# An adjacency-masked two-layer residual network on one core: the last group's work written out as one list of pieces

## The chip, the core and the metric

The kernel runs on one core of a Trainium2 chip. The core has five engines that work side by side, each through its own stream of instructions in order: TensorE (PE, matrix products; its weight loads are shown as PEld), VectorE (DVE), ScalarE (ACT), GpSimd (POOL) and SyncE (SP, which here issues the DMA transfers). An instruction that waits holds up everything behind it on its engine. The metric is the device time of one execution in microseconds (us); lower is better.

## What is computed

There are 128 graphs ("batches") of 128 nodes with 512 features each, and one 128x128 adjacency matrix per graph. Both layers are applied to every batch, each with a residual and a layer norm:

```python
# layer 0: 8-head attention under the adjacency mask
q, k, v = (x @ W + b for each of Wq, Wk, Wv)          # 128x512 @ 512x512
logits = einsum('bqhd,bkhd->bhqk', q, k) / sqrt(64)
attn = softmax(where(adj > 0, logits, -1e9), axis=-1)
out = einsum('bhqk,bkhd->bqhd', attn, v) @ Wo + bo
x = layernorm(x + relu(out))
# layer 1: additive graph attention, softmax over the first node index
Wh = x @ W1
e = leaky(s_i[:, :, None] + s_j[:, None, :])          # s_i, s_j = Wh @ a1, Wh @ a2
att = softmax(where(adj > 0, e, -9e15), axis=1)
x = layernorm(x + leaky(att @ Wh))
```

All of it is float32. The batches don't depend on each other; within a batch everything is one long chain.

## The kernel before

**Tiles and products.** Four batches form a group. The Q, K and V products of a group (`products`, L371) and the two 512x512 products of a pair of batches (`pair_product`, L420, for the output projection with `wo` and for `W1`) are done by one level of Strassen's scheme: seven products of half size, p1, p5, p6, p2, p7, p4, p3 (`strassen`, L283). Three of them (p1, p6, p7) are copied out of the accumulator banks by ScalarE into the tiles `t0`, `t2`, `t3` (`st_t` for a group, `pr_t` for a pair, L443), since the bank is then written again by the next product; VectorE adds these to the banks to form the blocks of the result. The block sums of the left operand are made on GpSimd (`left_blocks`, L269, four operations, L276 to L279).

**A batch's way.** Layer 0: scores (L476, banks `lg`), mask added and maximum taken on VectorE (L485, L491), eight exponentials and eight divisions on ScalarE (`exp` L497, `divide` L511, tile `pa`), the result stored to DRAM (L518) and fetched back in another order by four transfers (L522, tile `paz`), turned on VectorE (L526, `paT`), the product with V (`attend`, L539), copied to `oT` on ScalarE (L552), the projection with `wo` for the pair, the residual (L586) and the norm. The norm is `norm_stats` (L565: statistics on VectorE, L567 and L569, then the inverse root on GpSimd, L572 and L574) and `normalize` (L577: one VectorE operation, L578). The normalized tile `x1` is stored (L594), fetched back by four transfers (L240), turned on VectorE (L245, `x1T`). Layer 1: the product with `W1` for the pair, the edge softmax (`EdgeSoftmax`, L645: two turns on TensorE, L652 and L653, then L655 to L672 on ScalarE and VectorE), the product with the attention (L681), a copy to `z` on ScalarE (L685), leaky and residual on VectorE (L689, L690), a norm of the same kind (L578) and the store of the output (L697).

**Order.** All engines run in the order in which the program is written (`manual_schedule`, L710). A software pipeline sets it: step `t` of the loop at L782 does the first softmax of batch `t`, the attention product of batch `t-1`, the output projection of the pair that begins at `t-3` (odd `t`) or the `W1` product of the pair at `t-6` (even `t`), the edge softmax of batch `t-7`, the end of batch `t-8`, and a few pieces of the Q, K, V products of a later group (`group_steps`), which are all done by the end of step 124. The loop runs to `t = 136`, 128 batches and 9 steps more; in the last steps whatever has no batch left is skipped, and the rest keeps its order and place in the step.

**Buffers.** Tiles come from pools with a few buffers per name. In the stretch of interest: one buffer each for `pa`, `paz`, `paT`, `oT`, `x1T`, `z`, `y` and for each of the three copies `pr_t`; one for `e`, two for `att`, three for the small statistics; five accumulator banks for `lg`, `p_oT`, `p_e`, `p_h` and the pair products, three more for the group products.

Of the kernel before, what the change touches and what calls it, by code (L numbers as in the profile page):

```python
# [8 lines left out]
F32 = mybir.dt.float32  # L9
# [15 lines left out]
def kernel(  # L25
# [206 lines left out]
    X, XT, XS, Q, K, V, MF, PA, OT, X1T, X1, WH, ATT = ({} for _ in range(13))  # L232
# [31 lines left out]
    def sum_x(g):  # L264
        sums = big.tile([P, 3, 2, 2 * P], F32, name="xS")
        XS[g], add = left_blocks(XT[g], sums)
        return add

    def left_blocks(xT, sums):  # L269


        xt = xT.rearrange("p (i c) (h t) -> p i h c t", i=2, h=2)
        a11, a12, a21, a22 = (xt[:, i, h] for h in range(2) for i in range(2))

        def add():
            nc.gpsimd.tensor_add(sums[:, 0], a21, a22)  # L276
            nc.gpsimd.tensor_sub(sums[:, 1], sums[:, 0], a11)
            nc.gpsimd.tensor_sub(sums[:, 2], a11, a21)
            nc.gpsimd.tensor_sub(a21, a12, sums[:, 1])  # L279

        return (a11, a12, a21, a22, sums[:, 0], sums[:, 1], sums[:, 2]), add

    def strassen(bank, multiply, read, add):  # L283

        p, t = {}, {}

        def p1():  # L290
            p["y"] = bank("y")
            multiply(p["y"], 0, True)
            t[0] = read("t0", p["y"], 0)

        def p5():
            p["w"] = bank("w")
            multiply(p["w"], 4, True)

        def p6():
            multiply(p["y"], 5, False)  # L300
            t[2] = read("t2", p["y"], 1)

        def p2():
            p["x"] = bank("x")
            multiply(p["x"], 1, True)
            add(0, 0, p["x"], t[0])

        def p7():
            multiply(p["y"], 6, False)
            t[3] = read("t3", p["y"], 1)  # L310
            add(1, 1, p["w"], t[3])

        def p4():
            multiply(p["y"], 3, False)
            add(1, 0, p["y"], None)

        def p3():
            multiply(p["w"], 2, False)
            add(0, 1, p["w"], t[2])

        return [p1, p5, p6, p2, p7, p4, p3]
# [49 lines left out]
    def products(g):  # L371
# [20 lines left out]
        chains = [  # L392
# [3 lines left out]
        ]  # L396

# [20 lines left out]
        return order + chains[2][5:]  # L418

    def pair_product(xs, w, add, bias=None):  # L420
# [3 lines left out]
        def multiply(p, n, start):  # L424
# [6 lines left out]
            for kc in range(2):  # L431
                nc.tensor.matmul(  # L432
                    p[:, :width],
                    xs[n][:, kc, :],
                    w[:, PLACE[n], kc, :],
                    start=start and kc == 0,
                    stop=True,
                    skip_group_check=True,
                )

        def read_out(name, p, o):
            t = work.tile([P, HALF + 1], F32, name=f"pr_{name}")
            nc.scalar.copy(t[:, :width], p[:, :width])  # L443
            return t[:, :width]

        return strassen(
            lambda role: psum(f"p_{role}"),
# [17 lines left out]
    class Softmax:  # L465


        def __init__(self, b):
            self.b = b
            q, k = (a[b // GROUP, b % GROUP // 2] for a in (Q, K))  # L470
# [9 lines left out]
        def maxima(self):  # L480
            self.pa = work.tile([P, 4, H, 32], F32, name="pa")
            by_head = self.pa.rearrange("p b h k -> p h b k")
            mf = MF[self.b].rearrange("p (b k) -> p b k", b=4)
            for r in range(2):
                nc.vector.tensor_add(  # L485
                    by_head[:, r * NC : (r + 1) * NC],
                    self.lg[r].rearrange("p c (b k) -> p c b k", b=4),
                    mf.unsqueeze(1).to_broadcast([P, NC, 4, 32]),
                )
            self.nmax = small.tile([P, H], F32, name="nmax")  # L490
            nc.vector.tensor_reduce(self.nmax, by_head, AX.XY, ALU.max, negate=True)  # L491
            self.sums = small.tile([P, H], F32, name="sums")
            self.rs = small.tile([P, H], F32, name="rs")
# [21 lines left out]
        def spread(self):  # L515

            d = dram.tile([P, 4, H * 32], F32, name="pa_dram")
            nc.sync.dma_start(d, self.pa.rearrange("p b h k -> p b (h k)"))  # L518
            self.paz = work.tile([P, 4, H * 32], F32, name="paz")
            block = d.rearrange("(a i) b e -> b i a e", i=32)  # L520
            for k in range(4):
                nc.sync.dma_start(self.paz[32 * k : 32 * k + 32], block[k])  # L522

        def transpose(self):
            self.paT = work.tile([P, H, P], F32, name="paT")
# [5 lines left out]
    def attend(sm):  # L531

        b = sm.b
        v = V[b // GROUP, b % GROUP // 2][:, b % 2, :]
        p = psum("p_oT").rearrange("p (c q) -> p c q", c=NC)
        for c in range(NC):
            for r in range(2):
                h = 2 * c + r
                nc.tensor.matmul(  # L539
                    p[r * HD : (r + 1) * HD, c, :],  # L540
                    v[:, h * HD : (h + 1) * HD],
                    sm.paT[:, r * NC + c, :],
                    start=True,
                    stop=True,
                )
        pair, h = divmod(b, 2)

        def copy():
            if h == 0:
                OT[pair] = work.tile([P, NC, 2 * P], F32, name="oT")  # L550
            for c in range(NC):
                nc.scalar.activation(  # L552
                    OT[pair][:, c, h * P : (h + 1) * P],
                    p[:, c, :],
# [3 lines left out]
            if h == 1:  # L558
                sums = work.tile([P, 3, 2, P], F32, name="oS")
                OT[pair], add = left_blocks(OT[pair], sums)  # L560
                add()

        return copy

    def norm_stats(src):  # L565
        st = small.tile([P, 6], F32, name="st")
        nc.vector.bn_stats(st, src)  # L567
        mv = small.tile([P, 2], F32, name="mv")
        nc.vector.bn_aggr(mv, st)  # L569
        with tc.high_priority(offset=400):  # L570
            ve = small.tile([P, 1], F32, name="ve")
            nc.gpsimd.tensor_scalar_add(ve, mv[:, 1:2], EPS)  # L572
            rstd = small.tile([P, 1], F32, name="rstd")
            nc.gpsimd.tensor_tensor(rstd, ve, mhalf, ALU.pow)  # L574
        return mv[:, 0:1], rstd

    def normalize(dst, stats):  # L577
        nc.vector.tensor_scalar(dst, dst, stats[0], stats[1], ALU.subtract, ALU.mult)  # L578

    def project_o(pair):  # L580

        y = {}

        def residual(b, o, src):
            dst = X1[b][:, o * HALF : (o + 1) * HALF] if o is not None else X1[b]
            nc.vector.scalar_tensor_tensor(dst, src, 0.0, dst, op0=ALU.max, op1=ALU.add)  # L586

        stats, d = {}, {}

        def store(h):  # L590
            b = 2 * pair + h
            normalize(X1[b], stats[h])
            d[h] = dram.tile([P, D], F32, name="x1_dram")
            nc.sync.dma_start(d[h], X1[b])  # L594

        def spread_both():
            store(0)
            for h in (1, 0):
                X[2 * pair + h, 1] = spread(d[h])

        def add(h, o, p, t):
            b = 2 * pair + h
            if h == 0:
                if o == 0:
                    y[0] = work.tile([P, D], F32, name="y")
                nc.vector.tensor_add(y[0][:, o * HALF : (o + 1) * HALF], p, t)
                if o == 1:
                    residual(b, None, y[0])
                    stats[0] = norm_stats(X1[b])
                    store(1)  # L610
                    later.append(spread_both)
            elif o == 1:
                nc.vector.tensor_add(t, p, t)
                residual(b, 1, t)
            else:
                residual(b, 0, p)
                stats[1] = norm_stats(X1[b])

        return pair_product(OT.pop(pair), wo, add, bias_rows)

    def transpose_x1(b):
        pair, h = divmod(b, 2)
        if h == 0:
            X1T[pair] = work.tile([P, NC, 2 * P], F32, name="x1T")
        transpose_blocks(X1T[pair][:, :, h * P : (h + 1) * P], X.pop((b, 1)))
        if h == 1:
            sums = work.tile([P, 3, 2, P], F32, name="x1S")
            X1T[pair], add = left_blocks(X1T[pair], sums)
            add()

    def project_w(pair):

        for h in range(2):
            WH[2 * pair + h] = work.tile([P, 2, HALF + 1], F32, name="wh", bufs=4)

        def add(h, o, p, t):
            dst = WH[2 * pair + h][:, o, :]
            if t is None:
                nc.scalar.copy(dst, p)
            else:  # L640
                nc.vector.tensor_add(dst, p, t)  # L641

        return pair_product(X1T.pop(pair), w1, add)

    class EdgeSoftmax:  # L645


        def __init__(self, b):
            self.b = b
            s = WH[b][:, :, HALF : HALF + 1]  # L650
            self.p = psum("p_e").rearrange("p (c k) -> p c k", c=NC)
            nc.tensor.transpose(self.p[:, 0, :], s[:, 0, :].to_broadcast([P, P]), ident)  # L652
            nc.tensor.transpose(self.p[:, 1, :], MF.pop(b), ident)  # L653
            self.e = small.tile([P, P], F32, name="e", bufs=1)
# [273 lines left out]
```

## Time and profile before

| | us |
|---|---|
| median of 3 runs | 2503.51 (2501.39 to 2504.53) |
| the profiled execution | 2503.92 |
| its span, first to last instruction | 2502.1 |
| first scores of batch 124 on TensorE (L476) start at | 2359.49 |
| scores of batches 125, 126, 127 start at | 2379.53, 2393.67, 2410.37 |
| last product (L681) starts at | 2492.49 |

The span counts from the first instruction to the last; the device time lies 1.8 us around it. From 2359.5 us on, the last group's first scores, there are 142.6 us left. Busy time in that stretch: PE 99.03, DVE 92.88, ACT 55.11, POOL 39.23 us. A record of "x8" on TensorE is eight passes; a float32 product is shown as two passes, so "x4" of L432 is one of the seven products of a pair.

### The profile page before, as it was taken

Reading aid. Unit: us, or ns where it says so; the run is one execution under the profiler, and the core shown is the slowest. Engines: PE = TensorE matmul, PEld = TensorE weight load, DVE = VectorE, ACT = ScalarE, POOL = GpSimd, SP = SyncE. Lnnn points to the kernel's source line nnn. Section 1 sums busy time; section 2 is a strip of 40 time slices with the busy share of each in tenths; the row PEclk is TensorE's granted clock in tenths of the full one; section 3 lists DMA queues with packets and bytes.
Section 4 is the critical chain, followed back from the end, with each engine's and each line's share of the span. In section 5 each row is a group of like instructions: output and inputs, shape, how many; then the busy total and the mean of one; then the engine's idle time right before and its main releaser. Section 6 shows DMA issues by size and latency. Waiting matters only on the chain.

```text
span 2502.1 us, 43770 instructions
## 1 busy us (share of the span) xinstructions
PE 2438.1 (97%) x13713; PEld 2006.4 (80%) x13713; DVE 1815.5 (73%) x3757; ACT 1429.1 (57%) x5188; POOL 779.0 (31%) x1161
## 2 busy tenths in 40 slices
PE   8899999999999999999999999999999999999975
PEld 6688888888888888888888888888888888888853
DVE  6667776777776777776777777777777777777675
ACT  2565565565565565556566556556556556556551
POOL 2222323322323323323323323323333323333232
PEclk9999999999999999999999999999999999999987
DMA  6544544544544544544544544544544444544441
GB/s 191 179 140 143 164 154 144 170 151 144 162 146 156 168 149 146 165 146 151 169 145 152 164 144 152 168 145 150 166 149 152 163 144 152 164 150 147 151 133 47
DMA packets 351112, 379.92 MB, mean 152 GB/s; under 512 B 38936, under 2 KB 255008, under 8 KB 350880
## 3 DMA queue, kind: packets, MB, share of 16 engines
q1 hardware_dynamic: 350016, 376.07, 46.9%
q8 instruction: 110, 1.80, 0.3%
q10 hardware_dynamic: 864, 1.05, 0.1%
q14 instruction: 122, 1.00, 0.1%
HBM read 240.91 MB, written 136.05 MB: 151 GB/s over the span
## 4 chain that ended last, share of the span: by engine, by line
PE 93%; DVE 2%; issue 1%; ACT 1%; DMA 1%; POOL 1%; SPq 0%; POOLq 0%; DVEq 0%; ACTq 0%
PE st_y L349 26%; PE p_y L432 17%; PE st_w L349 13%; PE p_w L432 9%; PE st_x L349 7%; PE lg L476 5%; PE p_oT L539 5%; PE p_h L681 4%; PE p_x L432 4%; PE p_e L653 1%; PE p_e L652 1%; DMA wv_n<-wv 1%; ACT pa L497 0%; DVE st L567 0%; ACT pa L511 0%
## 5 line engine op out<-in xcount | busy, mean ns | idle before, releaser
L572 POOL TENSOR_SCALAR ve<-mv 128x1 f32<-128x1 f32 x256 | 68.5, 267 | 1376.1 <-DVE mv L569 1376.1
L497 ACT ACTIVATE pa<-pa,nmax 128x128 f32<-128x128 f32 x1024 | 398.9, 392 | 47.6 <-DVE nmax L491 36.4
L511 ACT ACTIVATE pa<-pa,rs 128x128 f32<-128x128 f32 x1024 | 336.5, 395 | 30.0 <-DVE rs L507 30.0
L552 ACT ACTIVATE oT<-p_oT,b_cols 128x128 f32<-128x128 f32 x512 | 145.3, 366 | 201.5 <-PE p_w L432 199.4
L485 DVE TENSOR_TENSOR pa<-lg,mf 128x512 f32<-128x512 f32 x256 | 164.4, 684 | 99.4 <-PE lg L476 96.9
L326 ACT COPY st_t<-st_y 128x512 f32<-128x512 f32 x192 | 110.6, 576 | 157.4 <-PE st_y L349 157.4
L476 PEld LDWEIGHTS lg<-kT,qT 64*128 64x128 f32 x2048 | 124.3, 188 | 93.6 <-issue 93.6
L497 ACT ACTIVATION_READ_ACCUMULATOR pa<-pa,nmax 128x1 f32 x1024 | 194.1, 190 | 0.0
L574 POOL TENSOR_TENSOR rstd<-ve,mhalf 128x1 f32<-128x1 f32 x256 | 176.5, 690 | 21.3
L443 ACT COPY pr_t<-p_y 128x256 f32<-128x256 f32 (+1 forms) x384 | 140.3, 365 | 71.0 <-PE p_y L432 67.6
L526 DVE STREAM_TRANSPOSE paT<-paz 128x1024 f32<-128x1024 f32 x128 | 159.3, 1245 | 1.0 <-issue 0.3
L491 DVE TENSOR_REDUCE nmax<-pa 128x8 f32<-128x1024 f32 x128 | 156.2, 1220 | 4.4
L681 PE MATMUL p_h<-wh,att 128*128 128x512 f32 x256 | 133.9, 605 | 17.5 <-DVE att L672 17.5
L539 PEld LDWEIGHTS p_oT<-paT,v 128*64 128x64 f32 x2048 | 111.8, 139 | 47.2 <-issue 42.1
L476 PE MATMUL lg<-kT,qT 64*128 64x128 f32 x2048 | 148.8, 285 | 0.0
L539 PE MATMUL p_oT<-paT,v 128*64 128x128 f32 x2048 | 143.1, 283 | 3.2 <-DVE paT L526 3.2
L330 ACT ACTIVATE st_t<-st_y,b_cols 128x256 f32<-128x256 f32 x192 | 80.5, 470 | 114.1 <-PE st_y L349 114.1
L432 PE MATMUL p_y<-w,x1S 128*128 128x257 f32 x512 | 134.0, 384 | 10.3 <-ACT pr_t L443 10.3
L641 DVE TENSOR_TENSOR wh<-p_w,pr_t 128x257 f32<-128x257 f32 x128 | 54.1, 423 | 122.4 <-PE p_w L432 73.1
L432 PE MATMUL p_y<-wo,oS 128*128 128x256 f32 x512 | 133.6, 384 | 6.7 <-ACT pr_t L443 6.7
L655 ACT ACTIVATE e<-p_e,wh 128x128 f32<-128x128 f32 x128 | 47.3, 369 | 161.4 <-PE p_e L653 161.4
L432 PE MATMUL p_y<-w,x1T 128*128 128x257 f32 x512 | 134.7, 386 | 1.0 <-ACT pr_t L443 1.0
(151 smaller groups left out, 5961.1 us busy)
## 6 DMA issues: line engine op xcount, KB each, us to landing
pa_dram<-pa SPq DMA_DIRECT2D x128, 512.0 KB, 2.6
paz<-pa_dram SPq DMA_DIRECT2D x512, 128.0 KB, 2.7
wv_n<-wv SPq DMA_DIRECT2D x224, 256.0 KB, 2.9
x<-in_x_dram SPq DMA_DIRECT2D x128, 256.0 KB, 2.9
x_dram<-x SPq DMA_DIRECT2D x128, 256.0 KB, 2.3
xz<-x_dram SPq DMA_DIRECT2D x512, 64.0 KB, 2.0
out_dram<-z SPq DMA_DIRECT2D x128, 256.0 KB, 2.4
xz<-in_x_dram SPq DMA_DIRECT2D x496, 64.0 KB, 2.2
```

Of the source, the lines that this page charges most:

```text
L349: nc.tensor.matmul(p[:, m, :], lhs, rhs, start=start and m == 0 and kc == 0, stop=True, skip_group_check=True,)
L432: nc.tensor.matmul(p[:, :width], xs[n][:, kc, :], w[:, PLACE[n], kc, :], start=start and kc == 0, stop=True, skip_group_check=True,)
L476: nc.tensor.matmul(self.lg[r][:, c, :], q[rows, c, cols], k[rows, c, cols], start=True, stop=True)
L485: nc.vector.tensor_add(by_head[:, r * NC : (r + 1) * NC], self.lg[r].rearrange("p c (b k) -> p c b k", b=4), mf.unsqueeze(1).to_broadcast( ...
L491: nc.vector.tensor_reduce(self.nmax, by_head, AX.XY, ALU.max, negate=True)
L497: nc.scalar.activation(self.pa[:, :, h, :], self.pa[:, :, h, :], AF.Exp, bias=self.nmax[:, h : h + 1], accum_out=self.sums[:, h : h + 1],)
L511: nc.scalar.activation(self.pa[:, :, h, :], self.pa[:, :, h, :], AF.Copy, scale=self.rs[:, h : h + 1])
L526: nc.vector.transpose(self.paT.rearrange("p h (a i) -> p a h i", i=32), self.paz.rearrange("p a (h k) -> p a h k", k=32),)
L539: nc.tensor.matmul(p[r * HD : (r + 1) * HD, c, :], v[:, h * HD : (h + 1) * HD], sm.paT[:, r * NC + c, :], start=True, stop=True,)
L552: nc.scalar.activation(OT[pair][:, c, h * P : (h + 1) * P], p[:, c, :], AF.Identity, bias=b_cols[:, 1, c : c + 1],)
L574: nc.gpsimd.tensor_tensor(rstd, ve, mhalf, ALU.pow)
L681: nc.tensor.matmul(p.rearrange("p (o f) -> p o f", o=2), edge.att, wh, start=True, stop=True)
```

## The change

The loop now ends after step 123 (`END = B - GROUP`). Everything after it, from the last six V products and the first scores of batch 124 on, is a list of 428 named pieces, `PLAN`, which is run through in order and so gives the order on every engine. To make that possible the functions are taken apart into methods, one for each piece: `strassen` returns a dictionary of products, copies and blocks, and `in_order` puts them together again as before for the loop; `Softmax`, `LayerZero`, `LayerOne`, `Edge` and `Norm` have a method for each step.

In the list `s0` to `s3` are the softmaxes of batches 124 to 127 (`sl` is 123's), `v` the V product of the last group, `al`, `a0`, `a1`, `a2` the output projections and norms of pairs 60 to 63, `b0` to `b4` the `W1` products of pairs 59 to 63, `e0` to `e10` the edge softmaxes and ends of batches 117 to 127 (`el` is 116's), `x` and `m` the loads of residual rows and masks.

Tiles in the list get buffers in places that no later batch needs: the weights `wq` and `wk`, and the buffers of `xT`, `xS`, `qT` and `kT`. So `pa`, `paz`, `paT`, `oT` and `x1T` have two places each, `z`, `e` and `att` four each, the pair copies two sets, and the `W1` products from `b1` on use the three banks of the group products. The small statistics have four buffers in place of three and the DRAM tile `x1_dram` four in place of three, throughout the kernel.

In the list 18 of the 19 norms (all but the first, `al.apply.0`) are applied on ScalarE, `x * rstd + shift`, with `shift = -mean * rstd` made by two more GpSimd operations.

```diff
+        def rstd(self):
+            ve = small.tile([P, 1], F32, name="ve", bufs=4)
+            nc.gpsimd.tensor_scalar_add(ve, self.mv[:, 1:2], EPS)
+            self.r = small.tile([P, 1], F32, name="rstd", bufs=4)
+            nc.gpsimd.tensor_tensor(self.r, ve, mhalf, ALU.pow)
+            if self.on_scalar:
+                minus = small.tile([P, 1], F32, name="minus", bufs=4)
+                nc.gpsimd.tensor_scalar_mul(minus, self.mv[:, 0:1], -1.0)
+                self.shift = small.tile([P, 1], F32, name="shift", bufs=4)
+                nc.gpsimd.tensor_tensor(self.shift, minus, self.r, ALU.mult)
+
+        def apply(self):
+            if self.on_scalar:
+                nc.scalar.activation(
+                    self.src, self.src, AF.Identity, bias=self.shift, scale=self.r
+                )
+                return
+            nc.vector.tensor_scalar(
+                self.src, self.src, self.mv[:, 0:1], self.r, ALU.subtract, ALU.mult
+            )
...
-    for t in range(-3, B + 9):
+    END = B - GROUP
+    for t in range(-3, END):
...
+    homes = [
+        {"oT": spare("kT", 3)},
+        {"pa": spare("xT", 2), "paz": spare("xS", 2), "paT": spare("qT", 4)},
+        {},
+        {"pa": spare("xT", 2), "paz": spare("xS", 2), "paT": spare("qT", 4)},
+    ]
...
+        jobs[f"b{n}"] = LayerOne(
+            END // 2 - 3 + n, home=home, bank=end_bank if n else None
+        )
+    z_homes = [None, block(wq, 4), block(wq, 5), block(wq, 6)]
...
+    PLAN = """
+        v.p5 x0.x el.residual m1.adj s0.scores m2.adj v.fetch al.apply.0 x1.x b0.p1
+        sl.transpose al.fetch.1 v.p6 b0.t0 s0.add.0 m1.cast s0.add.1 m3.adj al.store.0
+        s1.scores s0.reduce v.t2 v.fetch v.p2 m1.mask s0.exp.4.5 s1.add.0 s1.add.1 s0.exp.6.7
...
+        v.c12 s2.exp.2.3 el.store s3.scores e0.maxima s2.exp.6.7 s1.fetch sl.attend e0.exp
+        s2.exp.4.5 e0.divide e1.turn b1.p5 s0.transpose sl.copy e0.product m3.cast
...
+        b2.t3 e3.store e4.add b2.p4 a2.stats.0 a2.apply.1 b2.c22 a2.rstd.0 b2.c21 a2.store.1
+        b2.c11 b2.p3 a1.transpose.0 e6.turn e4.maxima a2.apply.0 a1.sum.0 b3.p1 e6.add
+        a2.store.0 a1.sum.1 b2.c12 b3.p2 e4.exp e6.maxima b3.t0 a2.fetch.1 a1.sum.2 e5.turn
...
+        e7.residual e9.product e8.apply e10.copy e8.store e7.stats e9.copy e10.residual e7.rstd
+        e10.stats e7.apply e9.residual e7.store e10.rstd e9.stats e10.apply e10.store e9.rstd
+        e9.apply e9.store
+    """
+    for piece in PLAN.split():
+        name, method, *numbers = piece.split(".")
+        getattr(jobs[name], method)(*map(int, numbers))
```

## The prediction

> **What bounds the kernel now.** I read the page first (busy shares), then the busy time by stretches, then the waits of the last stretch.
>
> ```profile
> PE 2438.1 (97%) x13713; PEld 2006.4 (80%) x13713; DVE 1815.5 (73%) x3757; ACT 1429.1 (57%) x5188; POOL 779.0 (31%) x1161
> ...
> 2285.90:2359.50 73.60, 73.60 (x412) 60.80 (x410) 53.22 (x111) 43.87 (x161) 23.20 (x34) 1.00 0.45 145
> 2359.50:2502.10 142.60, 99.03 (x467) 72.37 (x466) 92.88 (x208) 55.11 (x196) 39.23 (x66) 0.84 0.31 101
> ```
>
> The columns of a stretch are its length, then busy PE, PEld, DVE, ACT, POOL, the granted clock, the DMA share and GB/s. Over four steps before the last group PE has no idle time at all: there only fewer or faster products could help, and the change touches neither. Behind 2359.5 us PE is idle for 43.6 of 142.6 us and its clock falls to 0.84. The chain of waits names what stands behind the idle time; columns are start, length, what:
>
> ```profile
> 2385.22 0.30 DVE nmax L663
> 2385.54 0.50 ACT att L667 x2
> 2386.04 0.77 ACT pa L497 x4
> 2386.80 0.26 ACT pr_t L443
> ...
> 2387.20 1.98 PE p_y L432 x4
> ```
>
> PE needs the copy `pr_t`, which frees its bank. The copy needs 0.26 us, but is written behind exponentials of the step and behind the edge softmax's exponential, which waits for VectorE. While group products were there, PE had other work; now it stands. The waits of PE in this stretch (total, times, longest) are these two and 0.4 us:
>
> ```profile
> PE p_y L432 <- ACT pr_t L443: 18.2, 9, 4.6
> PE p_h L681 <- DVE att L672: 17.5, 3, 6.6
> ```
>
> The rest, some 7.5 us, lies behind the last product. So the end is bound by order and by round trips, not by an engine's work.
>
> **The work that is left.** What the list must do on PE I count at the rate of the undisturbed stretch:
>
> ```profile
> 2299.97 1.73 PE st_y L349 x8
> ...
> 2303.42 0.86 PE p_h L681 x2
> 2304.28 1.09 PE lg L476 x16
> ...
> 2307.62 0.87 PE p_y L432 x4
> ...
> 2315.51 1.02 PE p_oT L539 x16
> ```
>
> Six V products at 1.73 (10.4), four scores at 1.09 (4.4), five attends at 1.02 (5.1), 56 pair products at 0.86 (48.2), six bias products at 0.11 (0.7), eleven edges at 0.22 for the turns and 0.86 for the product (11.9): 80.7 us. The 99.03 busy us of before are these and 18.3 us of slow clock: the product at 2387.20, behind a wait of 2.47 us, took 1.98 instead of 0.86.
>
> VectorE, by the rows of the same stretch: 12 residuals at 1.38 (L689 and L690, medians), 18 statistics at 0.87, 11 edge maxima at 0.96, 11 edge divisions at 0.44, 8 mask adds at 0.684, 4 maxima at 1.22, 8 reciprocals at 0.15, 5 turns at 1.245 and 8 at 0.67, 15 blocks of the `W1` products at 0.42, 2.8 for each of three pairs in layer 0, 3 V blocks at 0.69, 3 masks at 0.28, one norm at 0.53: 89.0 us. As neighbours overlap in the record, the other way to count is busy time less what leaves: 92.88 - 18 x 0.531 = 83.3 us. I take 89.0, by which no overlap is assumed, and keep 83.3 for the low end.
>
> **The change part by part.** *The loop up to step 123.* Each engine's instructions stand there in the same order as before; four small buffers for three can only take waits away, and PE has none. Price nothing; if it were not so, one per cent of PE time there would be 24 us.
>
> *The norms.* VectorE loses 18 x 0.531 = 9.6 us, ScalarE and GpSimd gain work:
>
> ```profile
> L685 ACT COPY z<-p_h 128x512 f32<-128x512 f32 x12 | 7.1, 588 | 24.8 <-PE p_h L681 24.8
> L578 DVE TENSOR_SCALAR z<-z,mv,rstd 128x512 f32<-128x512 f32 x12 | 6.4, 531 | 7.4 <-POOL rstd L574 7.4
> L574 POOL TENSOR_TENSOR rstd<-ve,mhalf 128x1 f32<-128x1 f32 x19 | 12.2, 643 | 1.6
> L572 POOL TENSOR_SCALAR ve<-mv 128x1 f32<-128x1 f32 x19 | 4.9, 260 | 76.0 <-DVE mv L569 76.0
> ```
>
> A 512-wide ScalarE operation with bias and scale is not in the trace. Below it stands the plain copy at 0.588, above it two 256-wide operations with bias (L330, 0.470 each), 0.94. I take 0.67: L330, and 0.2 for the second half, by which copies grow from 256 (0.365) to 512 columns (0.576). That is 12.1 us (10.6 to 16.9) on ScalarE, 55.1 to 67 of over 100 us: hidden. `minus` is of L572's kind, 0.26; `shift` lies between L572 and L574, 0.26 to 0.64, taken at 0.45. GpSimd goes from 39.2 to 52 us, hidden too. On each norm's way out the sum is +0.26 + 0.45 + 0.67 - 0.55 = 0.8 us. It is cover for 17 norms and is paid at the last: from the last aggregate (2497.40 + 0.18) to the end the trace has 4.5 us, now 5.4 (0.52 less without `shift`'s upper half, 0.5 more with the dear ScalarE operation).
>
> One rule speaks against this move. The Trainium skill's page "ScalarE: Activation LUTs", section "Rules for kernel authors", sends additions and multiplications to VectorE; its section "What ACT_TABLE_LOAD costs" gives 186 ns, 93 for each pointer operand and 0.833 a column, from which I estimate 0.80 us, 0.71 behind a neighbour. The row agrees that VectorE is faster for one operation (0.531 here). By that page ScalarE would gain 12.8 us in place of 12.1, and by its rule, norms left on VectorE, the sum below would be 9.6 us longer.
>
> *The order.* Where is the list bound? Up to the scores of batch 127 it holds 10.4 + 4.4 + 6.0 (`b0`) + 1.7 (two of `b1`) + 0.2 = 22.7 us for PE and 17.6 for VectorE. PE leads there, and VectorE can't run ahead of the scores and products it waits for. Behind that place 58 us are left for PE, 71.4 for VectorE. So VectorE takes over as the bound, and the least time is 22.7 + 71.4 + 5.4 = 99.5 us. With the other count of VectorE (66.8 left) it is 94.9.
>
> Does any batch's way take longer? For batch 127, from its scores: softmax 9.4 (exponentials 0.39 apart, divisions 0.31), store and fetch 7.4, turn, attend, copy and sums 6.3, projection and norm 11.4, store and fetch of x1 6.4 (store 0.4 + 2.0, four issues 2.0, landing 2.0), turn and sums 3.6, `W1` product 7.5, edge and end 11.7: 63.7 us. With 21.6 ahead of it that ends at 85, 14 us below the bound.
>
> *Transfers.* 84 transfers stand on SP's queue behind the same place as before; a fetch waits there for its store, and every later transfer behind it. The tightest place is pair 63: from `a2.stats.0` to `a2.transpose.0` the list gives VectorE 8.8 us of other work, while rstd, shift, application, store and fetch need 0.9 + 0.7 + 0.67 + 2.4 + 4.0 = 8.7. Pairs 61 and 62 have 11.8 and 11.2. So the fetches cost nothing by this sum, and up to 2.6 us each where the cover slips.
>
> *Waits that stay.* Each edge makes a round trip from VectorE to ScalarE and back between maximum and division; where nothing stands between, it costs 0.6 us (2489.70 to 2490.3), and for `e0` both stand side by side in the list. I allow 11 x 0.6 = 6.6, and one fetch late by 2.0: 8.6 us. Ends: nothing, and 23 (second rival). The clock costs little, since PE has 13 us to spare behind the first part.
>
> **The sum.** 99.5 + 8.6 = 108 us in place of 142.6, 34.5 less. The profiled execution, 2503.92 with its 1.8 us around the span, would be at 2469.4; the median shown is 0.41 lower: 2469. Its own range is 2459 (the low count of VectorE, 4 us of waits) to 2478 (17 us of waits).
>
> **Rivals.** *Fetches take the place of the copies.* Behind the scores of batch 127 there are nine fetches; each that is uncovered stops SP and then VectorE for its store's landing, 2.6 us at most. For it:
>
> ```profile
> SPq L522 <- DMA pa_dram<-pa: 10.2, 4, 3.6
> SPq L240 <- DMA x_dram<-x: 3.1, 5, 1.6
> ```
>
> SP does stand for landings today. Against it is the cover above. Nine times 2.6 is 23.4: 99.5 + 23.4 = 123, a gain of 19.7, 2484.
>
> *No gain.* The end would be bound by one batch's way. The 63.7 us speak against it: it would have to be 120. Within 5 us of 2503.5.
>
> *Slower: ScalarE's queue.* The list holds 24 copies `t0`, `t2`, `t3`, each of which holds PE's next product of the chain, and ScalarE, in order, now also has 18 norms that wait for GpSimd. If every copy stood behind something that waits, as the long ones do today (2.47, 4.61, 2.88, 2.89, 2.83, mean 3.1), that is 75 us on 99.5: 174.5, 2535. It decides from (142.6 - 99.5) / 24 = 1.8 us a copy. For it: that is today's main wait. Against it: in the list two chains of products alternate nearly everywhere, so that PE has the other chain's product while one waits, and ScalarE has a third of its time free.
>
> **How the numbers follow.** First forecast 0.70, below its range 0.06, fetches 0.16, no gain 0.03, slower 0.05. A difference of 0.2% (5 us) is about what a measurement of this kernel can tell from no change; so faster 0.92, within 0.03, slower 0.05. The range goes from 2459 to 2486, the fetch case and 2 us.
>
> **What would show it.** Right: unchanged first 2359 us; behind them DVE the busiest engine, at 83 to 89 us, PE near 81 and its clock above 0.95, PE's waits for `pr_t` below 6 us, no L681 slower than 1.1 us but the last. The scores of batch 127 start near 20 us behind those of 124 (51 now). Wrong: VectorE idle in front of the turns of `paz` or `xz` for more than 10 us (fetches), PE idle in front of `p_y` for more than 15 us (ScalarE's queue), an application on ScalarE above 1 us, or a first part that is longer.

## The result and the profile after

| | median, us | range of the runs | ratio to before |
|---|---|---|---|
| before | 2503.82 (4 runs) | 2501.39 to 2504.53 | |
| changed | 2466.44 (4 runs) | 2463.92 to 2468.18 | 0.9852 [0.9835, 0.9869] |

The changed kernel is faster by 37.4 us, 1.5%. Its profiled execution took 2466.47 us, 2.1 of them around the span. From the page of the changed kernel, the span and the busy time of each engine:

```profile
span 2464.4 us, 43800 instructions
...
PE 2425.7 (98%) x13713; PEld 1996.7 (81%) x13713; DVE 1807.8 (73%) x3739; ACT 1441.2 (58%) x5206; POOL 788.8 (32%) x1197
```

PE is less busy by 12.4 us with the same 13713 instructions: of the 18.3 us of slow clock behind its waits about two thirds are gone. VectorE has 18 instructions fewer, ScalarE 18 more, GpSimd 36 more; these are the norms. The busy time by stretches of the changed kernel (columns as in the prediction: length, then busy PE, PEld, DVE, ACT, POOL, granted clock, DMA share, GB/s) says where the time came from:

```profile
2285.30:2358.90 73.60, 73.60 (x412) 60.82 (x410) 53.20 (x111) 43.87 (x161) 23.20 (x34) 1.00 0.45 146
2358.90:2464.40 105.50, 86.52 (x467) 64.61 (x466) 85.45 (x190) 66.98 (x214) 49.40 (x102) 0.94 0.41 137
2358.90:2382.80 23.90, 23.75 (x153) 19.61 (x154) 17.73 (x34) 18.31 (x71) 5.06 (x10) 1.00 0.60 196
2382.80:2458.90 76.10, 62.77 (x316) 45.00 (x316) 67.72 (x156) 47.04 (x143) 43.13 (x88) 0.95 0.36 122
```

The first row is the same four steps as before, and the same: 73.60 us, PE never idle. All the gain is in the second row, 105.5 us where 142.6 stood, a difference of 37.1. PE and VectorE are both busy for about 86 of the 105.5 us, and neither fills them. PE's waits in that stretch (total, times, longest):

```profile
PE p_h L803 <- DVE rt L797: 3.1, 1, 3.1
PE p_y L452 <- ACT wk L463: 1.7, 2, 1.0
PE p_y L452 <- ACT pr_t L463: 1.1, 1, 1.1
...
PE p_h L803 <- DVE wk L798: 0.7, 1, 0.7
PE p_y L452 <- POOL shift L637: 0.6, 1, 0.6
```

The two waits that were 18.2 and 17.5 us are 2.8 (the copies now go to `pr_t` or to `wk`) and 3.8 (`rt` and `wk` of the edge softmax). The last row, 0.6 us, is put down to GpSimd's `shift`, which PE doesn't read; the product in question starts at 2404.89, 0.15 us after a copy to `pr_t` ended, so it is more likely a third wait for a copy. The scores of the last group, by start and length, first and last of four in PE's timeline:

```profile
2360.73 1.16 PE L504 MATMUL lg<-kT,qT 64*128 64x128 f32 x16
...
2381.61 1.16 PE L504 MATMUL lg<-kT,qT 64*128 64x128 f32 x16
```

Batch 127 starts 20.9 us behind batch 124; before it was 50.9. So the last batch's way begins 30 us earlier, counted from batch 124's scores, while PE still has full work.

The chain of waits gives a first idea of what holds the end now (start, length, what; "issue" is time for which it shows no wait). It is PE, all but without a break, until 2392.5, then VectorE for 2.5 us, and from 2395.1 to 2404.9 this:

```profile
2394.94 0.19 DVE mv L626
...
2398.63 0.23 POOL minus L635
2398.95 0.19 POOL shift L637
2399.13 0.69 POOL spare L275
...
2399.89 0.73 POOL spare L276
2400.62 1.13 POOL spare L277
...
2401.84 0.23 POOL ve L630
...
2402.14 0.64 POOL rstd L632
...
2404.71 0.20 POOL shift L637
2404.93 0.82 ACT x L641
```

The small operations of two norms, the block sums `spare` of a pair product, and the small operations of two more norms stand in one queue on GpSimd, each started as the one before ends, and the last norm's application on ScalarE waits behind them all. Summed by engine, the listed pieces of this chain from 2358.9 on are PE 37.9, GpSimd 22.3, VectorE 20.8, ScalarE 3.1, and 15.3 of issue, much of it the 0.07 us between GpSimd's small operations and a single stretch of 6.8 behind a `shift`. That stretch is GpSimd standing idle for VectorE, as its own waits say:

```profile
POOL ve L630 <- DVE rt L797: 6.8, 1, 6.8
```

There the listed chain follows GpSimd's order past the work that it waited for, and 9.6 of GpSimd's 22.3 us lie from 2439.8 us on, around that idle time. So the share of over a fifth shows where to look, in an engine that is busy for 49.4 of 105.5 us, and not what GpSimd costs; for that the runs below added work to it.

### The profile page after: what moved, and what is told of

The parts are those of the page before. It is cut to its first block, busy times and chain, and to the rows that moved or that the text cites. A ratio compares the mean times of both kernels' runs of the same rounds, so it can differ in the third digit from the quotient of the medians.

```text
span 2464.4 us, 43800 instructions
## 1 busy us (share of the span) xinstructions
PE 2425.7 (98%) x13713; PEld 1996.7 (81%) x13713; DVE 1807.8 (73%) x3739; ACT 1441.2 (58%) x5206; POOL 788.8 (32%) x1197
## 4 chain that ended last, share of the span: by engine, by line
PE 93%; DVE 2%; issue 2%; POOL 1%; ACT 1%; DMA 1%; SPq 0%; DVEq 0%; POOLq 0%; ACTq 0%
PE st_y L366 27%; PE p_y L452 17%; PE st_w L366 14%; PE p_w L452 9%; PE st_x L366 7%; PE lg L504 5%; PE p_oT L581 5%; PE p_x L452 4%; PE p_h L803 4%; PE p_e L776 1%; PE p_e L777 1%; ACT pa L533 0%; POOL rstd L632 0%; ACT pa L547 0%; PE p_y L447 0%
## 5 line engine op out<-in xcount | busy, mean ns | idle before, releaser
L533 ACT ACTIVATE pa<-pa,nmax 128x128 f32<-128x128 f32 x1008 | 392.7, 393 | 42.5 <-DVE nmax L522 34.4
L547 ACT ACTIVATE pa<-pa,rs 128x128 f32<-128x128 f32 x1008 | 331.4, 395 | 30.0 <-DVE rs L543 30.0
L513 DVE TENSOR_TENSOR pa<-lg,mf 128x512 f32<-128x512 f32 x252 | 161.8, 683 | 97.9 <-PE lg L504 95.4
L463 ACT COPY pr_t<-p_y 128x257 f32<-128x257 f32 (+1 forms) x375 | 137.1, 366 | 63.6 <-PE p_y L452 60.5
L581 PE MATMUL p_oT<-paT,v 128*64 128x128 f32 x2016 | 137.9, 279 | 3.2 <-DVE paT L568 3.2
L452 PE MATMUL p_y<-w,x1T 128*128 128x257 f32 x496 | 128.5, 381 | 2.5 <-ACT wk L463 1.7
L452 PE MATMUL p_y<-wo,oT 128*128 128x256 f32 x504 | 129.5, 379 | 0.0
L366 PE MATMUL st_y<-wv_n,xS 128*128 128x256 f32 x512 | 124.6, 386 | 3.7 <-ACT pa L547 2.8
```

Source lines behind the costliest of these rows:

```text
L366: nc.tensor.matmul(p[:, m, :], lhs, rhs, start=start and m == 0 and kc == 0, stop=True, skip_group_check=True,)
L452: nc.tensor.matmul(p[:, :width], xs()[n][:, kc, :], w[:, PLACE[n], kc, :], start=start and kc == 0, stop=True, skip_group_check=True,)
L513: nc.vector.tensor_add(by_head[:, r * NC : (r + 1) * NC], self.lg[r].rearrange("p c (b k) -> p c b k", b=4), mf.unsqueeze(1).to_broadcast( ...
L533: nc.scalar.activation(self.pa[:, :, h, :], self.pa[:, :, h, :], AF.Exp, bias=self.nmax[:, h : h + 1], accum_out=self.sums[:, h : h + 1],)
L547: nc.scalar.activation(self.pa[:, :, h, :], self.pa[:, :, h, :], AF.Copy, scale=self.rs[:, h : h + 1])
L581: nc.tensor.matmul(self.oT[r * HD : (r + 1) * HD, c, :], v[:, h * HD : (h + 1) * HD], self.paT[:, r * NC + c, :], start=True, stop=True,)
```

## The experiments

Twelve kernels, each beside runs of the kernel before on the same chip. Ratios are against those, with their 95% interval. "List" is the changed kernel's order, "loop" the old one, run to the end over the last group too.

| run | order | what differs | median, us (range) | ratio |
|---|---|---|---|---|
| e1 | list | norms on VectorE | 2467.08 (2466.48 to 2470.54) | 0.9859 [0.9846, 0.9872] |
| e2 | loop | norms on ScalarE | 2509.55 (2507.06 to 2512.79) | 1.0027 [1.0018, 1.0036] |
| e3 | loop | the list's places | 2503.07 (2499.11 to 2504.53) | 0.9999 [0.9991, 1.0008] |
| e4 | loop | pair steps ahead of the exponentials | 2501.16 (2497.48 to 2505.58) | 0.9990 [0.9982, 0.9999] |
| e5 | list | `shift` in one operation | 2464.11 (2463.43 to 2467.00) | 0.9851 [0.9834, 0.9867] |
| e6 | list | 12 us more for GpSimd | 2475.74 (2473.36 to 2476.64) | 0.9894 [0.9879, 0.9908] |
| e7 | list | e5, 10 of 18 norms on VectorE | 2466.12 (2464.51 to 2466.75) | 0.9856 [0.9841, 0.9870] |
| e8 | list | e5, 12 of 18 norms on VectorE | 2466.83 (2466.61 to 2467.07) | 0.9859 [0.9845, 0.9874] |
| e9 | list | 9.6 us more for VectorE | 2468.21 (2465.97 to 2469.54) | 0.9859 [0.9845, 0.9874] |
| e10 | list | 14.6 us more for ScalarE | 2470.28 (2468.45 to 2471.80) | 0.9868 [0.9852, 0.9885] |
| e11 | list | e1, 12 us more for GpSimd | 2469.85 (2467.63 to 2470.93) | 0.9866 [0.9851, 0.9881] |
| e12 | list | e1, 9.6 us more for VectorE | 2473.91 (2472.95 to 2474.72) | 0.9884 [0.9868, 0.9901] |

### The three parts of the change, apart

**e1**, the list with its 18 norms on VectorE:

```diff
-    fin.on_scalar = True
...
-        jobs[f"a{n}"] = LayerZero(END // 2 - 1 + n, extra, on_scalar=True)
+        jobs[f"a{n}"] = LayerZero(END // 2 - 1 + n, extra)
...
-            on_scalar=True,
```

> The list as it stands, with all 19 norms of the list applied on VectorE at the same places in the order (no minus, no shift). Theory of the prediction (VectorE is the bound behind the first 23 us): VectorE gets up to 18 x 0.531 = 9.6 us back, 2471 to 2476 us. Rival (what VectorE saves is given back to GpSimd's queue, where each norm has two more operations, and to the dearer ScalarE operation, 0.81 measured): 2463 to 2469 us.

It keeps 35.8 of the 37.4 us (2502.89, the kernel before beside it, less 2467.08), and differs from the changed kernel by 0.6 us of median, less than either range is wide. The step "norms left on VectorE, the sum would be 9.6 us longer" fell. Its profile has the 10 us more of VectorE work and 7 us less of GpSimd work in the tail:

```profile
2358.90:2468.70 109.80, 87.99 (x473) 65.54 (x471) 95.89 (x211) 55.35 (x199) 42.12 (x68) 0.95 0.41 136
```

(This profiled execution is the longest of e1's runs.) Its chain, summed as above, is VectorE 53.5, PE 19.9, GpSimd 5.6: another engine holds the end, at nearly the same time. From its chain, start, length, what:

```profile
2424.59 0.43 DVE wq L645
2425.03 0.34 DVE x L666
2425.39 0.70 DVE st L624
...
2426.22 0.51 DVE wq L645
```

VectorE goes from norm (L645) to sum to statistics with no gap worth naming.

**e2**, the norms alone: the old loop and buffers (but for the small statistics' four), ScalarE for the same 18 norms.

```diff
-            pair_steps = zero[(t - 3) // 2] = LayerZero((t - 3) // 2)
+            pair_steps = zero[(t - 3) // 2] = LayerZero((t - 3) // 2, on_scalar=t > END)
...
-            edge = Edge(t - 7) if on(t - 7) else none
+            edge = Edge(t - 7, on_scalar=t >= END) if on(t - 7) else none
```

> The loop's old order and old buffers to the end, with only the 18 norms of the last steps applied on ScalarE. Theory (the end is bound by order, VectorE has slack there): no gain, each norm's way 0.8 to 1 us longer, 2501 to 2510 us. Rival (the norms bring a good part of the gain): below 2495 us.

Slower by 6.7 us: in the loop's order the copies of `pr_t` stand on ScalarE behind these norms too, and PE's wait for them is 21.4 us in 14 places, 18.2 in 9 before. That is 3.2 us of it; the rest is not traced to a wait.

**e3**, the places alone: the list's buffers, handed out in the old loop.

```diff
-        last, sm = sm, Softmax(t) if on(t) else none
+        last, sm = sm, Softmax(t, homes[t - END] if t >= END else None) if on(t) else none
...
-            edge = Edge(t - 7) if on(t - 7) else none
+            edge = edge_of(t - 7) if on(t - 7) else none
```

> The loop's old order with norms on VectorE, but with the list's places for the last batches' tiles (pa, paz, paT, oT, x1T, z, e, att, y, the pair copies, and the banks of the group products for the W1 products). Theory (the order holds the engines, not the buffers): within 4 us of before, 2500 to 2505. Rival (waits for buffers are a part of the idle time): 2495 us or less.

0.9999 [0.9991, 1.0008]: buffers alone bring nothing. PE's two waits are there as before, 18.4 us for the copies and 17.5 for the edge softmax.

Places alone bring 0, norms alone cost 6.7, and the list without the norms brings 35.8: the gain is the order, with the places that it needs. The order without the places wasn't tried: the list has exponentials of batch 125 (`s1.exp.4.5`) ahead of the store of batch 124 (`s0.store`), which one buffer of `pa` doesn't allow. What the order alone is worth is therefore not shown.

### Was it the copies behind the exponentials?

**e4**: the old loop, but in its last steps all three pair steps are issued ahead of the first exponential, so that no copy stands behind one.

```diff
-            pair()
+            pair(1 if t < END else 3)
             sm.exp(0, 1, 2, 3)
             edge.exp()
-            pair()
+            pair(1 if t < END else 0)
```

> The loop's old order, buffers and norms, with one thing changed in the steps from 124 on: the first three products of the pair (p1, p5, p6) and their two copies stand ahead of the first exponentials and the edge softmax's exponential. Theory (18.2 of the 43.6 idle us of TensorE are copies that stand behind exponentials): the waits of p_y for pr_t fall from 18.2 to under 6 us and the kernel gains 8 to 13 us, 2491 to 2496. Rival (the wait only moves to the next round trip): 2499 to 2506 us with new waits of the same sum elsewhere.

A gain of 2.5 us by the ratio (0.3 to 4.5) where 8 to 13 were expected. PE's waits behind 2359 us say why:

```profile
PE p_h L803 <- DVE att L798: 17.6, 3, 6.7
PE p_oT L581 <- DVE rs L543: 8.7, 3, 4.2
PE p_y L452 <- ACT pr_t L463: 4.7, 6, 1.9
PE p_oT L581 <- DVE paT L568: 3.3, 1, 3.3
PE p_w L452 <- DVE wh L751: 1.6, 1, 1.6
PE p_w L452 <- DVE pr_t L677: 1.1, 1, 1.1
```

The named wait did fall, from 18.2 to 4.7. But 12.0 us came back in front of the attends (`p_oT`), which wait for the softmax (`rs`, `paT`) now that the pair's work stands ahead of it, and the edge's 17.5 stayed (17.6). All of PE's waits together are 37.0 us, 36.1 before: the rival's case. With one step of the loop in this order, moving one wait away only made the next ones longer.

### What holds the end now?

**e5** gives GpSimd 18 operations less: both halves of `shift` in one instruction.

```diff
-                minus = small.tile([P, 1], F32, name="minus", bufs=4)
-                nc.gpsimd.tensor_scalar_mul(minus, self.mv[:, 0:1], -1.0)
...
-                nc.gpsimd.tensor_tensor(self.shift, minus, self.r, ALU.mult)
+                nc.gpsimd.tensor_scalar(
+                    self.shift, self.mv[:, 0:1], self.r, -1.0, ALU.mult, ALU.mult
+                )
```

> The changed kernel with shift = mean * rstd * -1 made by one GpSimd operation in place of two: 18 operations of 0.26 and their gaps of 0.07 less, about ten of them in the stretch in which GpSimd is busy without a break. Theory (GpSimd's queue and the longer way through it take what VectorE saves): 2461 to 2464.5 us. Rival (GpSimd has room; the norms bring nothing because VectorE isn't the bound either): 2465 to 2468 us.

2464.11 is the lowest median of all and inside the first expectation, but the ranges overlap and the ratios differ by 0.0001: inconclusive; the medians are 2.3 us apart.

**e6** adds two small operations to GpSimd for every ScalarE norm, 36 operations of about 0.26 us and 0.07 between them, some 12 us.

```diff
                 nc.gpsimd.tensor_tensor(self.shift, minus, self.r, ALU.mult)
+                for _ in range(2):
+                    nc.gpsimd.tensor_scalar_mul(self.shift, self.shift, 1.0)
```

> The changed kernel with two more GpSimd operations on shift (times one) in each of the 18 norms on ScalarE: 18 x 2 x 0.33 = 12 us more on GpSimd, 6.6 of them in the stretch in which it is busy without a break. Theory (GpSimd is part of what sets the end of the list): 5 to 10 us longer than the changed kernel, 2471 to 2477. Rival (GpSimd has room): at most the last norm's way, 0.7 us, 2465 to 2468.5.

9.3 us slower than the changed kernel by the medians, 10.5 by the ratios. "Hidden too" was wrong for GpSimd. PE's waits, of which the changed kernel has 8.8 us in all, are 13.3 here:

```profile
PE p_y L452 <- ACT wk L463: 4.0, 2, 2.1
...
PE p_y L452 <- POOL spare L277: 1.8, 1, 1.8
PE p_w L452 <- POOL x1S L275: 1.6, 1, 1.6
PE p_y L452 <- POOL minus L635: 1.3, 1, 1.3
PE p_y L452 <- POOL x1S L276: 0.8, 1, 0.8
PE p_w L452 <- POOL oS L275: 0.4, 1, 0.4
```

GpSimd reaches PE in two ways. The block sums `x1S` and `oS` stand behind the norms' small operations, and PE waits for them, 2.8 us. The copies stand on ScalarE behind applications that wait for `shift`: 4.0 for `wk`, and most likely also the two rows with `spare` and `minus`, whose products start at 2403.44 and 2406.81, each 0.14 to 0.15 us after a copy to `pr_t` ended. How the 9.3 us divide between the two ways is open.

**e7 and e8** take e5 and share the norms out: in e7 those of layer 0 and of the last four ends go to VectorE, in e8 only those of layer 0 stay on ScalarE.

```diff
-        jobs[f"a{n}"] = LayerZero(END // 2 - 1 + n, extra, on_scalar=True)
+        jobs[f"a{n}"] = LayerZero(END // 2 - 1 + n, extra)
...
-            on_scalar=True,
+            on_scalar=n < 7,
```

> The list with each norm where its engine has room: layer 0's norms (pairs 61 to 63) and the last four ends (batches 124 to 127) on VectorE, the other eight on ScalarE with the one shift operation. Theory (either engine alone is full, VectorE with all norms, GpSimd with the shifts): faster than the changed kernel and than the list with all norms on VectorE, 2458 to 2463 us. Rival (the order's round trips set the end, wherever the norms are): 2464 to 2468 us.

> The other way round: layer 0's six norms on ScalarE with the one shift operation, the twelve ends on VectorE. Theory: VectorE carries 12 x 0.53 = 6.4 us more in the full stretch, GpSimd 12 operations less: between the changed kernel and the list with all norms on VectorE, 2463 to 2468 us. If layer 0's way through DRAM and back sets the end, this is the slowest of the four, above 2468.

Neither is told apart from e1, e5 or the changed kernel. The gain of a few us that was expected of e7 was missed; e8 is where it was expected.

**e9, e10, e11 and e12** add known work to one engine at a time, with the norms on ScalarE (e9, e10) or on VectorE (e11, e12). The added VectorE and ScalarE operations work on a part of `wk` that nobody reads; GpSimd's in e11 are on `rstd`, as those of e6 are on `shift`.

```diff
+                idle = wk[:, 3].rearrange("p c f -> p (c f)")
+                nc.vector.tensor_scalar(idle, idle, 1.0, 0.0, ALU.mult, ALU.add)
```

> The changed kernel with one more VectorE operation beside each of the 18 applications on ScalarE: 128x512 on a place in wk that nothing reads, so no new dependence, 0.53 each, 9.6 us in all, just what the norms took off VectorE; GpSimd as in the changed kernel. Theory (VectorE sets the end behind the first 24 us, with 67.7 us of work in 76.1): 6 to 10 us longer, 2472 to 2476. Rival (VectorE's 8.4 idle us there take it up): 2467 to 2470 us.

> The changed kernel with each of the 18 applications followed by one more on that same unread place: 18 x 0.81 = 14.6 us more on ScalarE. Theory (ScalarE has room, 44 of 76 us): 0 to 4 us longer, 2466 to 2470. Rival (ScalarE's order holds the copies that TensorE waits for, the slower rival of the prediction): 2474 us or more.

> The list with all norms on VectorE, and two more GpSimd operations on rstd (times one) in each of 18 norms, the same 12 us that cost the changed kernel 9.3 to 10. Theory (where the norms stand decides which engine sets the end: with the norms on VectorE, GpSimd has 42 of 110 us and room): 0 to 4 us more than the list with norms on VectorE, 2467 to 2471. Rival (GpSimd's queue sets the end either way): 2474 us or more.

> The list with all norms on VectorE, and one more VectorE operation of 0.53 on the unread place in wk beside 18 of them, the same 9.6 us that cost the changed kernel 1.8. Theory (here VectorE has 95.9 of 109.8 us and sets the end): 6 to 10 us more than the list with norms on VectorE, 2473 to 2477. Rival (VectorE has room here too): 2467 to 2470.

What the same additions cost, by medians (by ratios in brackets):

| added to the tail | norms on ScalarE (changed) | norms on VectorE (e1) |
|---|---|---|
| some 12 us of GpSimd | +9.3 (10.5), e6 | +2.8 (1.8), e11 |
| 9.6 us of VectorE | +1.8 (1.8), e9 | +6.8 (6.3), e12 |
| 14.6 us of ScalarE | +3.8 (4.0), e10 | not run |

The busy time doesn't tell this. The tail of e9 and of e12:

```profile
2358.90:2467.40 108.50, 85.81 (x467) 64.44 (x466) 92.48 (x207) 66.91 (x214) 51.09 (x102) 0.94 0.41 133
```

```profile
2358.90:2471.30 112.40, 85.09 (x442) 64.22 (x440) 98.10 (x221) 53.48 (x195) 40.04 (x64) 0.93 0.37 124
```

In e9 VectorE has 7 us more than in the changed kernel, is by far the busiest engine, and the tail is 3 us longer in this execution: idle time took most of it. In e12 the same operations cost over three times as much by the medians (its tail stands only 2.6 us above the one shown for e1, as that execution was e1's longest). With the norms on ScalarE it is GpSimd's queue that the end feels, with the norms on VectorE it is VectorE's. (e9, e11 and e12 came out where their first or second expectation had them; e10, at 2470.28, a little past the top of its first and short of the 2474 that ScalarE's queue, holding the end, would have cost.) That the two ends lie within a microsecond or two of each other would explain why moving the norms shows nothing; it is inferred.

Two limits. GpSimd's added operations in e6 and e11 also make each norm's own way some 0.6 us longer, which the others don't: e6 alone can't tell a full queue from a longer way. In e11 the way is as much longer and costs 1.8 to 2.8 us, so the longer way is not enough by itself, but additions to GpSimd beside the norms' way weren't run. And the chains don't show these prices: GpSimd's listed part is 19.8 us in e6, where its additions cost most, and 26.6 in e11, where they cost little.

## Why the prediction was right

2469 was forecast and 2466.4 measured, inside the forecast's own range, and by the order, as forecast. Its terms against the trace of the changed kernel, the tail counted from 2358.9:

| term | predicted, us | measured, us |
|---|---|---|
| first part, to the scores of batch 127 | 22.7 | 23.9 |
| VectorE's work left | 71.4 (66.8 low) | 67.7 |
| waits | 8.6 | 8.4 (76.1 less 67.7) |
| end behind the last aggregates | 5.4 | 5.5 |
| tail | 108 | 105.5 |

**The first part** is PE's, as forecast: 23.75 of 23.9 us busy, clock 1.00.

**The mis-sized step is VectorE's work:** 89.0 us were taken, 85.45 measured. The count by medians took no overlap and erred by 3.6; the other, busy time less what leaves (83.3), erred by 2.2 to the other side. The 3.6 us are more than the whole error of the tail, 2.5; the first part, 1.2 us too short, offset some of it.

**"VectorE takes over as the bound"** is half of the truth. VectorE's work and its idle 8.4 us add up to the stretch by definition, and that the 8.6 fit doesn't show that VectorE sets the end; e9 and e6 show that it doesn't. The forecast's term for waits was made of edge round trips and one late fetch. The trace has 0.9 us of round trips (`rt` behind ScalarE) and one fetch late by 1.6; VectorE's largest wait is 2.2 us for one product. So the size came out, its parts did not. With the norms on VectorE (e1, e12) the sentence holds. That the sum came so near is in part luck: by the same sum the list with its norms on VectorE would take 9.6 us more, 2478.6, and it took 2467.1.

**"Norms: minus 9.6 us"** fell with e1. VectorE did lose the work, but what takes its place is as long: on each norm's way out, 0.81 + 0.26 + 0.28 us and the queue on GpSimd, for 0.53. The application was taken at 0.67 us, from copies and from a narrower operation with a bias alone (L330). (In the prediction's bracket on the end, 0.52 less and 0.5 more don't follow from the bounds beside them, 0.19 from 0.45 to 0.26 and 0.27 from 0.67 to 0.94; the sum doesn't use them.) From the groups of the tail of the changed kernel, x count, busy and mean ns, then idle time and what ended it:

```profile
L641 ACT ACTIVATE wq<-wq,shift,rstd 128x512 f32<-128x512 f32 x8 | 6.5, 810 | 8.5 <-POOL shift L637 6.4 <-DVE mv L626 2.1
...
L637 POOL TENSOR_TENSOR shift<-minus,rstd 128x1 f32<-128x1 f32 x18 | 5.0, 279 | 1.5
...
L635 POOL TENSOR_SCALAR minus<-mv 128x1 f32<-128x1 f32 x18 | 4.7, 264 | 1.2
```

The estimate of 0.80 us for a 512-wide operation with two pointer operands, from the figures of the Trainium skill's page "ScalarE: Activation LUTs" (section "What ACT_TABLE_LOAD costs"), is what was measured, 0.81; the neighbours were the wrong ones, a copy with no such operand at 0.588 and L330 with one. That page's other section, "Rules for kernel authors", would leave the norms on VectorE: here the two placements can't be told apart. The last column is the more telling one: ScalarE is idle in front of these applications for `shift`, that is, for GpSimd.

**GpSimd "hidden too"** fell with e6. The forecast compared 52 us of work with over 100 us of time. The work was right (49.4), the comparison was not: PE needs the block sums that are in the same queue, and the copies that stand behind applications waiting for it.

**The diagnosis of the kernel before,** PE behind copies behind exponentials, named a wait and not the cause. e4 removed 13.5 of its 18.2 us and got 2.5. The other half of the diagnosis, order and round trips rather than any engine's work, fits e1 to e3: another order, with room for it, took 36 us off.

**The signs that were named.** Met: the scores, the copies' waits below 6 us, the turns, an application below 1 us, the first 2359 us unchanged. Missed: PE is at 86.5 us instead of 81, its clock at 0.94, so VectorE is not the busiest; and not only the last edge product ran slow: the last two batches' products, four matmuls at 2451.11, took 3.16 us behind the wait of 3.1 us shown above.

**The rivals.** Fetches: VectorE's only wait for one is 1.6 us, not 23. (Its price of 2.6 us a fetch "at most" was the mean of the row that it showed, 10.2 us in 4; the longest there is 3.6.) Slower, by ScalarE's queue: 24 copies cost PE 2.8 us together (3.4 with the doubtful row), and 14.6 us more work on ScalarE (e10) cost 3.8, so it has room. In the old order the same mechanism is real (e2), which fits the condition of the rival, that nothing else is there for PE. No gain: refuted by the time.

**Open** is how much each part of the order brings, the earlier scores of batch 127 or the mixing of two pairs' products, and what would be next if both ends were shortened together; no version that was run beats the changed kernel by more than the runs scatter.

## What to carry to other kernels

Where a tail of in-order engines is bound by the order, one hoisted instruction group gives little, because its wait moves to the next one that finds no cover; the whole tail written as one interleaved list, with buffers for it, gave 36 us of 143. Ask of an engine that takes over work not only how many microseconds it has free, but which other instructions stand behind the new ones and who needs those: an engine that was busy for 49 us of 105 could not take 12 more without a price of 9 to 10. To find which engine sets an end, add the same known work to each in turn, if possible beside what others wait for; busy shares pointed at the wrong one here.

## What the runs showed of the hardware

Where a 128x512 operation of VectorE with two inputs from tiles (none from an accumulator bank) and a block sum of GpSimd overlap, both or one of them run slow. From the timeline of the changed kernel (start, length):

```profile
2411.72 0.69 DVE L624 BATCH_NORM_STATS2 st<-x 128x6 f32<-128x512 f32 x1
...
2412.49 0.73 POOL L276 TENSOR_TENSOR oS<-oS,oT 128x256 f32<-128x256 f32 x1
2412.61 1.15 DVE L813 SCALAR_TENSOR_TENSOR wq<-wq 128x512 f32<-128x512 f32 x1
2413.18 1.17 POOL L277 TENSOR_TENSOR oS<-oT 128x256 f32<-128x256 f32 x1
2413.80 1.10 DVE L814 TENSOR_TENSOR wq<-wq,x 128x512 f32<-128x512 f32 x1
...
2416.13 0.69 DVE L814 TENSOR_TENSOR wq<-wq,x 128x512 f32<-128x512 f32 x1
```

L813 and L814 take 1.10 to 1.20 us beside GpSimd's block sums and 0.69 without; the sum at L277 takes 1.17 beside them, and 0.73 is the usual length. In all nine overlaps of this kind in the tail (L666, L813 or L814 with a block sum) the one that started later is slow. The one-input statistics (L624) at 2411.72 ran at 0.69 beside a block sum, and so did L513, one of whose inputs is the bank `lg`, at 2385.90, beside sums of 0.73. GpSimd's small operations show it as well: `rstd` takes 0.57 us alone and 0.99 at 2397.57, behind the start of VectorE's L814 at 2397.44. The Trainium skill's page "GPSIMD Engine Reference" (section "Specifications") says that the two engines share their SBUF interfaces and that VectorE's instructions with two inputs in SBUF contend; these rows agree, and give the size. That the contention is what makes them slow is read from the overlaps and was not tested by itself.

The second is the price of a small GpSimd operation: on 128x1, 0.19 to 0.24 us undisturbed for `ve`, `minus` and `shift`, 0.57 for the power in `rstd`, and 0.07 us from each to the next, so that a norm's four small steps keep the engine for about 1.5 us.
